# Four closing units of matmuls in four iterations in a row, with the last overflow's sum ahead of the first

## The chip, the cores and the metric

The kernel runs on one core of one Trainium2 chip. The time is the device time of one execution in microseconds; lower is better. Before the change it is 2095.76 us, the median of three runs (2090.75 to 2101.2).

The engines named here are TensorE (PE in the profile; PEld is its loading of weights), VectorE (DVE), ScalarE (ACT), GpSimd (POOL) and SyncE (SP). Each takes its instructions in the order in which the program gives them, and waits on semaphores of the others. Transfers are issued on SP's queue, and the scatters on POOL's.

## The reference

One message-passing layer of a graph network, with 6250 nodes of 128 features and 200,000 edges, sorted by `dst`:

```python
h = jnp.maximum(_layernorm(x, axis=-1), 0.0)
xw = h @ W_in
W_ij = (shifted_softplus(f_ij @ W_f1 + b_f1) @ W_f2 + b_f2) * f_ij_cutoff
x_ij = xw[dst] * W_ij                                   # one row for each edge
agg = jax.ops.segment_sum(x_ij, src, num_segments=6250)
out = x + shifted_softplus(agg @ W_o1 + b_o1) @ W_o2 + b_o2
```

`f_ij` has 20 values for each edge, `f_ij_cutoff` one. The gather goes by the sorted index `dst`, the sum by the unsorted index `src`.

## The kernel before

**The loop.** Edges are taken in 391 quads of 512. An order written out by hand (a loop over an iteration number `i`, up to 404) puts the stages of several quads side by side: in iteration `i`, quad `i` enters its first layer, quad `i-1` its second, and so on. Other work hangs on hooks: `at(i, point, fn, ...)` files a function under an iteration and a point in it, and `run(i, point)` issues what is filed there, in the order of filing. The points of one iteration stand in the order L, D0, D1, A0, A1, DM, PE2, A2, D2, S. The instructions of an engine stand in the order in which the functions were issued.

**Two ways to sum.** 237 plain quads are summed by indirect DMAs that add rows to accumulators in DRAM (`scatter`, L421, 948 transfers on POOL's queue). The other 154 quads (`mpq`, gaps of 2 and 3) go another way. The edges of such a quad are sorted by a permutation matmul into 16 groups of nodes with 32 places each, 392 nodes to a group, and are kept as tiles `mst`. What finds no place in its group is overflow, up to 64 edges a quad.

**Units.** Eight quads form a round; the last round has ten (368 to 390). When its quads are sorted, a round is summed in four units `s`, each for four groups of nodes:

- `unit_oh` (L609), VectorE: for each quad a one-hot `so`, 128 x 392. There are ten buffers for `so`, so those of the next unit in the last round go into the same ten.
- `unit_pe` (L624), TensorE: for each quad, three parts of the values and four groups, a matmul of 32 rows by 392 columns; 120 in a unit of the last round. Four PSUM banks `un`, one for each group, collect them over the whole unit.
- `unit_evac` (L635), VectorE: four additions of the banks onto `accT`, the sum in SBUF.

They are filed at `k-1` D2, `k` PE2 and `k+1` D1, where `k` comes from `unit_slots`. For the last round, whose last quad is 390, the four `k` are 396, 398, 400 and 402.

**Overflow.** Two quads share one overflow (the last: 388 and 390). After the index (`over_idx`, L562) and a diagonal matrix `dg` (L567, ScalarE), `over_row` (L575, TensorE) makes `orow`; `over_eq` (L580, VectorE) compares it to `oeq`; `over_sum` (L585, TensorE) adds edges of the same node into `osum`; `over_copy` (L590, ScalarE), `over_ji` (L595, VectorE) and `over_int` (L599, ScalarE) make rows and index; `over_scatter` files one scatter. For quad 390 `over_row` is at 397 and `over_sum` at 399: `clear(i, units)` moves a number past iterations that have a unit. So on TensorE the order is unit 0, `orow`, unit 1, `osum`, unit 2, unit 3; on VectorE ten one-hots, four additions, ten one-hots, `oeq`, four additions, ten one-hots, `ojd`, four additions, ten one-hots, then two of the last four additions.

**PSUM.** `un`, `orow` and `osum` are tiles of one tag, "B", with four buffers that are given out in turn: a tile gets the bank of the tile four places before it, and its first matmul waits until that one has been read.

**Behind it.** The number of trips of a loop for edges outside of the gather windows is read on every engine (L1009), and the loop's branch (L1010) has a barrier of all engines, which also waits until the scatters have landed. Here there are no trips. VectorE's L1009 stands behind the second of the last four additions; the other two come after the branch. Then the tail loads the DRAM accumulators (L1080), adds them to `accT`, and does the two output layers for 13 groups of 512 nodes.

The places of the change, with the hooks of the units:

```python
                k = clear(q + 8, units)
                at(k, "PE2", over_sum, q)
...
            for s, k in enumerate(unit_slots(mpq, r)):
                at(k - 1, "D2", unit_oh, r, s)
                at(k, "PE2", unit_pe, r, s)
                at(k + 1, "D1", unit_evac, r, s)
```

Of the kernel before, what the change touches and what calls it, by code (L numbers as in the profile page):

```python
# [48 lines left out]
def tile_gnn(ctx: ExitStack, tc: tile.TileContext, x, fB, cT, srcT, srcr, dstr, win_, wf1, wf2, bias, bo1c, wo1,  # L49
# [25 lines left out]
    mpq = sorted_quads(NQ)  # L75
    mpi = {q: n for n, q in enumerate(mpq)}
    units = unit_its(mpq)
# [596 lines left out]
    with tc.manual_schedule():  # L674
# [106 lines left out]
        def at(i, point, fn, *a):  # L781
            hooks.setdefault((i, point), []).append((fn, a))
# [121 lines left out]
        for r in range(-(-len(mpq) // RKQ)):  # L904
            i = mpq[RKQ * r]
            at(i - 5, "D2", rank_group, r)
            k = clear(i - 4, units)
            at(k, "PE2", rank_count, r)
            at(k + 1, "D0", rank_own, r)
            k = clear(k + 1, units)  # L910
            at(k, "PE2", rank_over, r)
            at(k + 1, "D0", rank_slot, r)
        for q in mpq:
            at(q + 1, "D2", perm_oh, q)
            at(q + 2, "D2", part_rem, q, 1)
            at(q + 2, "D2", part_rem, q, 2)
            for s in range(4):
                at(q + 3 + s // 2, "PE2", permute, q, s)
                at(q + 4 + s // 2, "A0", perm_out, q, s)
            at(q + 4, "PE2", over_pe, q)  # L920
            at(q + 5, "A0", over_out, q)
            if q == mpq[-1] and mpi[q] % 2 == 0:
                at(q + 4, "D2", over_none, q)
            if mpi[q] % 2 or q == mpq[-1]:
                at(q + 5, "DM", over_idx, q)
                at(q + 6, "A0", over_dg, q)
                k = clear(q + 6, units)
                at(k, "PE2", over_row, q)
                at(k + 1, "D0", over_eq, q)
                k = clear(q + 8, units)  # L930
                at(k, "PE2", over_sum, q)
                at(k + 1, "A0", over_copy, q)
                at(k + 1, "DM", over_ji, q)
                at(k + 1, "A2", over_int, q)
                at(k + 1, "S", over_scatter, q)
        last = mpq[-1]
        for r in range(len(mpq) // RND):
# [4 lines that stand above are left out]
# [68 lines left out]
    with tc.For_i(0, trips, 1) as ci:  # L1010
# [49 lines left out]
        s = wk.tile([P, P], F32, bufs=1, tag="dg", name="fs")  # L1060
# [112 lines left out]
def sorted_quads(nq):  # L1173
    qs, q = [], MP0
    while q < nq - MPEND:
        qs.append(q)
        q += MPGAPS[(len(qs) - 1) % len(MPGAPS)]
    return qs if len(qs) % RND <= EXTRA else qs[:len(qs) // RND * RND]
# [7 lines left out]
def unit_slots(qs, r):  # L1186
    last = len(qs) // RND - 1
    nxt = [qs[n] + 2 for n in range(RND * (r + 1), min(RND * (r + 2), len(qs) if r < last else 0)) if qs[n] - qs[n - 1] == 3]
    return nxt[:4] if nxt else [qs[-1] + 6 + 2 * s for s in range(4)]


def unit_its(qs):
    return {i for r in range(len(qs) // RND) for i in unit_slots(qs, r)}


def clear(i, busy, n=1):
    while any(i + k in busy for k in range(n)):
        i += 1
    return i
# [114 lines left out]
```

## Time and profile before

| | |
|---|---|
| median of three runs | 2095.76 us |
| profiled execution, its own time | 2098.49 us |
| span of its instructions | 2096.7 us |
| mean granted clock of TensorE | 0.977 |
| busy share of the span: PE / DVE / ACT / POOL | 92 / 84 / 85 / 81 % |
| from the first matmul of the last round's unit 0 to the barrier's end | 2007.42 to 2041.90 us |
| from there to the end of the span | 54.8 us |
| last scatter issued on POOL until | 2035.32 us |

A line of the timeline gives start and length in us, engine, line of the kernel, operation, the tile written and the tiles read, shapes, and how often it came in a row; in brackets how long the engine was idle before it, and what ended that. Times of matmuls are modelled at their ends. A row of waits gives the total in us, how often, and the longest. A row of windows gives for a stretch the busy time of each engine with its count of instructions, the clock that TensorE was granted (1.00 is full), the share of the DMA engines and GB/s.

### The profile page before, as it was taken

The numbers are of one execution on the slowest core, as the hardware profiler recorded it, in microseconds if no ns is written. First come the engines' busy times: TensorE is split into PE (matmuls) and PEld (weight loads), VectorE is DVE, ScalarE is ACT, GpSimd is POOL, SyncE is SP. The second block draws the span as 40 slices with busy tenths as digits, with TensorE's granted clock in tenths as the row PEclk, the third lists the DMA queues.
The fourth block names the chain that finished last, engine by engine and source line by source line (L and its number), as shares of the span: only waits on it lengthen the run. The fifth ranks groups of instructions, "written<-read, shape, count | busy, mean of one in ns | idle before, by whom it ended". The sixth has DMA issues, their size and how long they took to land. (4 is left out here: it accounts for less than half of the span.)

```text
span 2096.7 us, 57222 instructions
## 1 busy us (share of the span) xinstructions
PE 1925.7 (92%) x19917; PEld 1404.4 (67%) x19917; DVE 1770.8 (84%) x4749; ACT 1792.0 (85%) x4789; POOL 1690.0 (81%) x1077
## 2 busy tenths in 40 slices
PE   3788999999999999998999999999999999999976
PEld 2566667676666667666667677776777776676744
DVE  4768888898989998888888989888988988888955
ACT  4688889898989888998889999989999998898824
POOL 3677888888888888888888888888888888888864
PEclk9789999999999999999999999999999999999997
DMA  7886667676667667766766776767776667667639
GB/s 260 211 167 112 126 112 128 121 126 123 117 124 128 113 119 131 124 117 124 132 115 113 123 121 120 118 119 119 119 127 118 126 111 123 117 114 138 127 37 241
DMA packets 377588, 270.57 MB, mean 129 GB/s; under 512 B 97199, under 2 KB 337242, under 8 KB 377298
## 3 DMA queue, kind: packets, MB, share of 16 engines
q0 software_dynamic: 149200, 73.79, 36.7%
q1 hardware_dynamic: 227810, 193.04, 33.2%
q8 instruction: 157, 2.57, 0.5%
q14 instruction: 133, 1.09, 0.2%
q10 hardware_dynamic: 288, 0.07, 0.0%
HBM read 153.14 MB, written 113.59 MB: 127 GB/s over the span
## 5 line engine op out<-in xcount | busy, mean ns | idle before, releaser
L421 POOL DMA_INDIRECT acc<-s,ji x948 | 1523.7, 1607 | 327.6 <-issue 217.8
L356 ACT ACTIVATE xc<-xg,cb 128x128 f32<-128x128 f32 x1564 | 446.5, 374 | 76.7 <-PE xg L343 59.9
L531 PE MATMUL pq<-pt,pm 128*128 128x387 bf16 x2464 | 485.7, 337 | 23.0 <-ACT s L381 13.0
L351 PE MATMUL W<-w,a 128*128 128x128 f32 x3128 | 463.6, 292 | 0.0
L351 PEld LDWEIGHTS W<-w,a 128*128 128x128 f32 x3128 | 388.0, 195 | 41.7 <-issue 2.0
L624 PE MATMUL un<-so,mst 32*128 32x392 bf16 x7392 | 358.7, 331 | 38.2 <-DVE pr L471 14.9
L531 PEld LDWEIGHTS <-pm 128*128 128x128 bf16 x2464 | 240.8, 98 | 184.1 <-issue 29.4
L624 PEld LDWEIGHTS <-mst 32*128 32x128 bf16 x7392 | 229.4, 94 | 162.8 <-issue 61.3
L328 DVE SCALAR_TENSOR_TENSOR a<-z,e 128x512 f32<-128x512 f32 x391 | 267.3, 684 | 64.2 <-ACT e L304 34.5
L304 ACT ACTIVATE e<-e,con 128x512 f32<-128x512 f32 x391 | 282.3, 722 | 12.7
L373 PEld LDWEIGHTS pp<-m,eq 128*128 128x128 f32 x1896 | 253.7, 196 | 35.0 <-DVE accT L635 15.8
L373 PE MATMUL pp<-m,eq 128*128 128x129 f32 x1896 | 260.6, 281 | 14.0 <-DVE accT L635 9.2
L537 ACT CAST mst<-pq 128x387 bf16<-128x387 f32 x616 | 264.2, 480 | 6.8 <-PE pq L531 5.6
L299 ACT ACTIVATE e<-e 128x512 f32<-128x512 f32 x391 | 246.5, 630 | 12.4
L298 ACT ACTIVATE e<-z 128x512 f32<-128x512 f32 x391 | 242.2, 620 | 15.1 <-PE z L293 14.6
L381 ACT COPY s<-pp 128x258 f32<-128x258 f32 x474 | 165.4, 392 | 67.0 <-PE pp L373 30.2
L361 DVE TENSOR_TENSOR m<-W,xc 128x512 f32<-128x512 f32 x237 | 162.5, 686 | 60.1 <-ACT xc L356 46.6
L521 DVE TENSOR_TENSOR pt<-pt 128x512 f32<-128x512 f32 x308 | 212.7, 691 | 0.0
L507 DVE TENSOR_SCALAR pm<-iot,pos 128x576 bf16<-128x576 f16 x616 | 201.4, 389 | 0.0
L635 DVE TENSOR_TENSOR accT<-un,accT 128x392 f32<-128x392 f32 x288 | 142.7, 558 | 45.7 <-PE un L624 28.2
L361 DVE TENSOR_TENSOR pt<-W,xc 128x512 f32<-128x512 f32 x154 | 106.1, 689 | 81.9 <-ACT xc L356 56.4
L293 PE MATMUL z<-ft,ws 123*128 123x512 bf16 x391 | 152.1, 389 | 14.9 <-POOL b2rep L763 9.2
(156 smaller groups left out, 2716.9 us busy)
## 6 DMA issues: line engine op xcount, KB each, us to landing
rb<-reld SPq DMA_DIRECT2D x391, 64.0 KB
fsd<-f SPq DMA_DIRECT2D x49, 480.0 KB
ft<-fsd SPq DMA_DIRECT2D x195, 120.0 KB
sb<-src SPq DMA_DIRECT2D x153, 128.0 KB
fb<-in_fB_dram SPq DMA_DIRECT2D x49, 320.0 KB
ft<-fsd SPq DMA_DIRECT2D x195, 80.0 KB
acc<-s,ji POOLq DMA_INDIRECT x948
wn<-tab SPq DMA_DIRECT2D x782, 15.8 KB
```

The lines of the kernel that those rows point to most:

```text
L298: nc.scalar.activation(e, st[q]["z"], AF.Abs)
L299: nc.scalar.activation(e, e, AF.Exp, scale=-1.0)
L304: nc.scalar.activation(e, e, AF.Ln, bias=half, scale=0.5)
L328: nc.vector.scalar_tensor_tensor(a, st[q]["z"], 0.0, st[q]["l"], op0=ALU.max, op1=ALU.add)
L351: nc.tensor.matmul(W[:, c, :], st[q]["a"][:, c * P:(c + 1) * P], w2, start=False, stop=(c == 3))
L356: nc.scalar.mul(xc[:, c, :], st[q]["xg"][:, c, :], late["c", q // CQ][:, 4 * (q % CQ) + c:4 * (q % CQ) + c + 1])
L361: nc.vector.tensor_tensor(m[:, :, :P], st[q]["W"], st[q]["xc"], op=ALU.mult)
L373: nc.tensor.matmul(pp[:, c, :129], st[q]["eq"][:, k, :], m[:, k, :129], start=True, stop=True)
L421: nc.gpsimd.indirect_dma_start(out=accs[k][:, :], out_offset=bass.IndirectOffsetOnAxis(ap=ji, axis=0), in_=s, in_offset=None, compute_op=A ...
L531: nc.tensor.matmul(t[:, :PW], mp[q]["pm"][:, c, s * P:(s + 1) * P], high(mp[q]["pt"][:, c:c + 1, :PW])[:, 0], start=(c == 0), stop=(c == 3))
L537: nc.scalar.copy(mp[q]["ms", s][:, :PW], mp[q].pop(("q", s))[:, :PW])
L624: nc.tensor.matmul(ts[g][:, :GN], mp[q]["ms", s][v, k * P:(k + 1) * P], mp[q]["oh"][v], start=(q == qs[0] and k == 0), stop=(q == qs[-1] a ...
```

## The change

Two lines. The last round's four units are filed at 397, 398, 399 and 400 in place of 396, 398, 400 and 402. And for the last quad, 390, `over_sum` is filed at `q + 7` = 397 without looking for an iteration that has no unit; hooks of one point run in the order of filing, and those of the overflow are filed first, so it stands before unit 0's matmuls. Since 396 no longer has a unit, `over_row` of quad 390 moves from 397 to 396.

```diff
-                k = clear(q + 8, units)
+                k = clear(q + 8, units) if q < mpq[-1] else q + 7
                 at(k, "PE2", over_sum, q)
                 at(k + 1, "A0", over_copy, q)
                 at(k + 1, "DM", over_ji, q)
...
-    return nxt[:4] if nxt else [qs[-1] + 6 + 2 * s for s in range(4)]
+    return nxt[:4] if nxt else [qs[-1] + 7 + s for s in range(4)]
```

The instructions are the same ones. On TensorE the order becomes `orow`, `osum`, unit 0, unit 1, unit 2, unit 3. On VectorE it becomes ten one-hots, `oeq`, ten one-hots, four additions, `ojd`, ten one-hots, four additions, ten one-hots, then six additions: the one-hots of a unit stand ahead of the additions of the unit before it. Up to quad 390's last sorting matmuls nothing moves, and the order on ScalarE, POOL and SP is what it was; VectorE's L1009 still stands behind the second of the last unit's additions.

## The prediction

> **What bounds the kernel now.** The change touches only the work after the last edges, so I asked first what that work holds up. The chain that ended last begins, in order of time, with the sync queue leaving the branch of L1010 and issuing the tail's loads of the accumulators (start us, us, what):
>
> ```profile
> 2041.90 0.02 SPq L1010
> ...
> 2042.18 0.37 SPq L1080
> ```
>
> So all that follows, 55 us up to 2096.7, is counted from 2041.90. The waits of the sync queue between 1990 and 2060 us say what it stood for there (total, times, longest):
>
> ```profile
> SPq L1010 <- DMA acc<-os,oji: 33.8, 1, 33.8
> SPq L1010 <- DVEq L1009: 3.9, 1, 3.9
> ```
>
> The last scatter had landed 3.9 us before the release, near 2037.9; what ended last was VectorE reaching its own L1009. VectorE alone, from 2006 to 2042 us (start, us, engine, line, operation, tiles, count, idle before and who ended it):
>
> ```profile
> 2006.99 2.52 DVE L609 TENSOR_SCALAR so<-iot,mst 128x392 bf16<-128x392 f16 x10
> 2012.77 1.98 DVE L635 TENSOR_TENSOR accT<-un,accT 128x392 f32<-128x392 f32 x4 [3.26 <-PE un L624]
> 2014.67 2.49 DVE L609 TENSOR_SCALAR so<-iot,mst 128x392 bf16<-128x392 f16 x10
> 2017.08 0.34 DVE L580 TENSOR_SCALAR oeq<-orow,ovs 128x128 f32<-128x128 f32 x1
> 2024.00 1.99 DVE L635 TENSOR_TENSOR accT<-un,accT 128x392 f32<-128x392 f32 x4 [6.57 <-PE un L624]
> 2033.36 1.99 DVE L635 TENSOR_TENSOR accT<-un,accT 128x392 f32<-128x392 f32 x4 [4.86 <-PE un L624]
> 2035.26 2.40 DVE L609 TENSOR_SCALAR so<-iot,mst 128x392 bf16<-128x392 f16 x10
> 2040.80 1.04 DVE L635 TENSOR_TENSOR accT<-un,accT 128x392 f32<-128x392 f32 x2 [3.13 <-PE un L624]
> ```
>
> One-hots, matmuls, additions, one unit after another; L1009 stands behind the second addition of the last unit, so the release comes 1.10 after 2040.80. TensorE in the same stretch:
>
> ```profile
> 2007.42 5.15 PE L624 MATMUL un<-so,mst 32*128 32x392 bf16 x120 [0.83 <-DVE so L609]
> 2013.49 0.46 PE L575 MATMUL orow<-dg,onesf 128*128 128x128 f32 x2 [0.92 <-DVE accT L635]
> 2015.04 0.34 PE L624 MATMUL un<-so,mst 32*128 32x392 bf16 x3 [1.09 <-DVE so L609]
> 2017.47 6.63 PE L624 MATMUL un<-so,mst 32*128 32x392 bf16 x117 [2.09 <-DVE oeq L580]
> 2024.62 0.49 PE L585 MATMUL osum<-mo,oeq 128*128 128x132 f32 x2 [0.51 <-DVE accT L635]
> 2026.27 6.84 PE L624 MATMUL un<-so,mst 32*128 32x392 bf16 x120 [1.15 <-DVE so L609]
> 2035.63 5.16 PE L624 MATMUL un<-so,mst 32*128 32x392 bf16 x120 [2.53 <-DVE so L609]
> ```
>
> Two things are to be seen. Unit 1 stops after three matmuls: its fourth tile gets the bank of `orow`, which `oeq` reads, and `oeq` stands on VectorE behind ten one-hots. And units 0 and 3 take 5.15 us (43 ns a matmul), units 1 and 2 about 1.6 more. The windows tell why (window, length, PE busy, PEld, DVE, ACT, POOL, granted clock, DMA); their edges are where the clock changed:
>
> ```profile
> 2013.80:2017.20 3.40, 0.49 (x5) 0.19 (x4) 3.40 (x14) 0.00 (x0) 2.79 (x3) 0.99 0.36 34
> ...
> 2024.00:2027.43 3.43, 1.76 (x31) 1.21 (x34) 3.43 (x11) 0.27 (x1) 2.82 (x3) 0.99 0.44 38
> 2027.43:2030.85 3.42, 3.42 (x51) 2.13 (x44) 1.07 (x5) 0.29 (x1) 2.81 (x3) 0.51 0.38 32
> ...
> 2034.26:2037.67 3.41, 2.04 (x52) 1.48 (x55) 3.40 (x13) 0.00 (x0) 1.07 (x1) 1.00 0.37 35
> 2037.67:2041.10 3.43, 3.12 (x76) 1.98 (x68) 0.30 (x1) 0.00 (x0) 0.00 (x0) 1.00 0.00 0
> ```
>
> The clock changes on a grid of about 3.41 us. After a window with 0.49 or 1.76 us of matmuls the next runs at half clock; after one with 2.04 it does not.
>
> **The change, step by step.** *The overflow's sum in front.* `orow` (L575) now comes before unit 0, `osum` (L585) directly behind it, and unit 0 behind both. `dg` ends on ScalarE at 2007.51 (row of L567: 2007.11, 0.40); `orow` takes 0.46, to about 2008.0. But `oeq` stands on VectorE behind unit 0's ten one-hots. Before, it began 2.41 after the first of the ten (2014.67 to 2017.08); so now 2006.99 + 2.41 = 2009.40, done with its 0.34 at 2009.74. `osum` starts 0.05 later, as the matmul of 2017.47 did after `oeq`: 2009.79. Unit 0's fourth tile takes the bank of `osum`, free when the copy `os` is done: it began 0.53 after `osum` (2024.62, 2025.15) and takes 0.27, so 2010.59. With 0.06 to react the fourth matmul stands at 2010.65, and the other work at full clock, 117 x 0.043 = 5.03, ends at 2015.68. Before it ended at 2012.57: **3.11 lost**. Cover for the ten one-hots is gone: TensorE used to work under them.
>
> *Units in a row.* The ten one-hots of the next unit now stand before the additions of this one. They write the ten buffers this unit reads, so the tenth waits for its last matmul, and the additions queue behind it. A cycle, from the last matmul of a unit to that of the next: 0.20 until VectorE reacts (2012.57 to 2012.77), 0.24 for the tenth one-hot, 1.98 for four additions, since the fourth matmul needs the fourth bank, 0.06, and 5.03: **7.51**. Before, from the additions of unit 2 to those of unit 3: 2040.80 - 2033.36 = 7.44. Nothing is won: the one-hots were hidden already, as the first was enough to start the matmuls, and the bound is the four banks.
>
> *The stall of unit 1* goes: it stopped between 2015.04 and 2017.47, worth 2.43 less 3 x 0.043 = **2.3 won**.
>
> *Scatter, copies, index.* `ojd`, `oji` and the scatter move forward, but POOL issues its queue back to back (1.85 each) in the same order until 2035.32, and no DMA changes place in it or on SP: nothing. If the index were late it would cost POOL only after 2033.78; it is ready some 10 us earlier.
>
> *Sum at full clock.* After: 2015.68 + 3 x 7.51 + 0.20 = 2038.41 for the last additions. Before, taking out the two slow units (6.63 - 5.03 = 1.60 and 6.84 - 5.15 = 1.69): 2040.80 - 3.29 = 2037.51. At equal clock the change loses 0.9.
>
> *The clock* is the unknown. I lay the new times on this profile's grid. Window 2006.97 to 2010.38 holds `orow`, `osum` and three matmuls, about 1.0 us: half clock until 2013.80, which takes 1.57 off unit 0's progress; it ends at 2017.26. The next window, to 2020.60, holds three trickling matmuls and 0.86 of unit 1, whose fourth is at 2019.74: about 1.0, so half clock until 2024.04, 1.72 lost, end 2026.46. Unit 2's fourth is at 2028.94; its window holds 2.0, nearest to the row with 2.04: held. End 2033.97. Unit 3's fourth is at 2036.45, its window has 1.35: half clock, 1.71 lost, end 2043.20. Additions at 2043.40: **2.6 later than 2040.80**. Bounds: no drop, 2038.41, 2.4 earlier; a drop in all four units, 6.7, so 2045.1, 4.3 later. Below, the landed scatter (2037.9) caps any gain at 3.9. I take 2.6: every gap between units is now some 2.4 us, and the gaps of 4.9 and 2.2 (with `osum` in it) dropped while that of 2.5 did not.
>
> The Trainium skill (TensorE: Matmul & The Clock Gate, HAM oscillation) gives as its rule that the clock falls after idle gaps of more than about 3.4 us. This trace differs: in the window that ended at 2027.43 no gap passed 1.15 us and the clock fell. By the rule, with `orow` and `osum` splitting the gap before unit 0, no unit would be slow and the last additions would stand at 2038.41; by the rows, at 2043.40. Its Part 1 says the grid runs free of the kernel, so another execution would lay it elsewhere; one profile here cannot show that.
>
> **The rivals.** *The clock holds.* For it: the gap of 2.53 before unit 3 cost nothing. Against: three new gaps and a worse one before unit 0. Price -2.4. *The clock drops in every unit* (slower): the place is each unit's first window, the price 1.6 to 1.7 each, 4.3 in all, decided where a window holds under some 1.8 to 2.0 us of matmuls; my unit 2 stands just on that edge. *Half clock throughout:* should no window reach the limit, 480 x 0.043 = 20.6 comes on top of 2038.41, 18.2 later. Against it: at half clock matmuls fill more of a window, and here every slow window was followed by a full one. *The stage is not the gate:* if the last scatter landed after VectorE, nothing would move; it had 3.9 us to spare.
>
> **How the numbers follow.** The profiled execution took 2098.49 with a span of 2096.7; the median of the three runs is 2095.76 (2090.75 to 2101.2), 2.7 below it. On that execution: 2096.7 + 2.6 = 2099.3 of span, 2101.1 in all; on the median 2098.4. About 0.5%, 10.5 us, is what a measurement of this kernel can tell from no change, and no likely case gets there. Chances: forecast (1 to 3.5 later) 0.60, 2098.4; clock holds 0.17, 2093.4; drops everywhere 0.18, 2100.1; half clock throughout 0.02, 2114; gate elsewhere 0.03, 2095.8. Range: 2093.4 less and 2100.1 plus 3, some half of the three runs' spread: 2090.5 to 2103. The forecast's own is 2094 to 2102. Chance of slower by over 0.5%: 0.05 (half clock, and a spread of runs on top of the late cases); faster 0.02 (spread alone, as 3.9 is the cap); same 0.93.
>
> **What would show it.** In the new profile `osum` at about 2.8 us after unit 0's first one-hot, unit 0's first matmul 3 us later than now, no stall on `oeq` inside a unit, four additions ending in each cycle of about 7.5 us where the clock is full, and at least two units with a half-clock window. Wrong it would be if TensorE started unit 0 before `osum`, if the next unit's matmuls began ahead of the additions, or if the release at L1010 were ended by the scatter.

## The result and the profile after

The changed kernel takes 2099.22 us, the median of 20 runs (2092.34 to 2103.41), against 2093.59 for the kernel before in 20 runs (2087.5 to 2101.2). The ratio is 1.0021 with a 95% interval of [1.0012, 1.003]: 4.4 us slower, 2.5 to 6.3 by the interval, which is less than the 0.5% that was taken as the bound of a change. The profiled execution took 2099.24, with a span of 2097.3.

The single spans say little, since one kernel's executions differ by more than ten microseconds. So I measure from a point inside: from the first of unit 0's one-hots (2006.99 before, 2006.03 after) to the start of the last unit's additions, called the stage here. It was 33.81 us and is 35.17.

The waits of the sync queue after, from 1990 to 2060 us (total, times, longest):

```profile
SPq L1010 <- DMA acc<-os,oji: 34.2, 1, 34.2
...
SPq L1010 <- DVEq L1009: 5.4, 1, 5.4
```

VectorE still ends last, and by 5.4 us where it was 3.9: the place of the bound is as forecast. VectorE after:

```profile
2006.03 2.52 DVE L609 TENSOR_SCALAR so<-iot,mst 128x392 bf16<-128x392 f16 x10
2008.47 0.34 DVE L580 TENSOR_SCALAR oeq<-orow,ovs 128x128 f32<-128x128 f32 x1
...
2017.52 1.96 DVE L635 TENSOR_TENSOR accT<-un,accT 128x392 f32<-128x392 f32 x4
...
2024.94 1.97 DVE L635 TENSOR_TENSOR accT<-un,accT 128x392 f32<-128x392 f32 x4
...
2034.16 1.96 DVE L635 TENSOR_TENSOR accT<-un,accT 128x392 f32<-128x392 f32 x4
2041.20 1.04 DVE L635 TENSOR_TENSOR accT<-un,accT 128x392 f32<-128x392 f32 x2 [5.07 <-PE un L624]
```

The first additions stand 11.49 us after the first one-hot, where before they stood 5.78 after it. From there on a cycle is 7.42 where the clock is full (2017.52 to 2024.94), as the last one was before (7.44). TensorE after:

```profile
2008.87 0.49 PE L585 MATMUL osum<-mo,oeq 128*128 128x132 f32 x2 [1.77 <-DVE oeq L580]
2009.29 0.34 PE L624 MATMUL un<-so,mst 32*128 32x392 bf16 x3
2010.36 6.81 PE L624 MATMUL un<-so,mst 32*128 32x392 bf16 x117 [0.73 <-ACT os L590]
...
2019.53 5.13 PE L624 MATMUL un<-so,mst 32*128 32x392 bf16 x117 [0.15 <-DVE accT L635]
...
2026.96 6.81 PE L624 MATMUL un<-so,mst 32*128 32x392 bf16 x117
...
2036.18 5.13 PE L624 MATMUL un<-so,mst 32*128 32x392 bf16 x117
```

`osum` comes 2.84 after the first one-hot, as forecast (2.8). But unit 0's fourth matmul comes 4.33 after it, not 3.66 as the prediction has it (2010.65 less 2006.99): the copy of the sum was late. ScalarE, and then GpSimd, in the same stretch:

```profile
2010.04 0.27 ACT L590 COPY os<-osum 128x132 f32<-128x132 f32 x1 [3.31 <-DMA acc<-os,oji]
```

```profile
2006.64 1.62 POOL L421 DMA_INDIRECT acc<-os,oji  x1 [0.30 <-ACT dg L567]
```

The copy waited for a DMA, not for the sum. `os` has two buffers, so the last overflow's rows go where those of the overflow of quads 378 and 380 lie, and that one's scatter, in the back of a full queue, was issued only at 2006.64 and had to land. Its issue ended at 2008.26, and the copy began 1.78 later. Units 0 and 2 are slow after the change, as units 1 and 2 were before. Windows on the clock's grid (columns as before):

```profile
2007.60:2011.00 3.40, 1.40 (x21) 0.87 (x25) 1.21 (x5) 0.27 (x1) 2.79 (x3) 1.00 0.33 25
...
2024.60:2028.00 3.40, 2.06 (x32) 1.02 (x34) 2.56 (x6) 0.00 (x0) 2.79 (x3) 1.00 0.44 38
...
2034.87:2038.30 3.43, 2.98 (x55) 1.73 (x57) 1.25 (x3) 0.00 (x0) 0.00 (x0) 1.00 0.16 17
```

After the first two the clock is half (0.50 and 0.51 in the window that follows), after the third it stays. 2.06 us of modelled busy time dropped here where 2.04 had held before; the count of matmuls separates these two better (32 against 52).

### The profile page after: what moved, and what is told of

It reads as the page before. It is cut to its first block, busy times and chain, and to the rows that moved or that the text cites. A ratio compares the mean times of both kernels' runs of the same rounds, so it can differ in the third digit from the quotient of the medians.

```text
span 2097.3 us, 57252 instructions
## 1 busy us (share of the span) xinstructions
PE 1926.7 (92%) x19917; PEld 1402.2 (67%) x19917; DVE 1777.3 (85%) x4749; ACT 1794.7 (86%) x4789; POOL 1688.1 (80%) x1077
## 5 line engine op out<-in xcount | busy, mean ns | idle before, releaser
L609 DVE TENSOR_SCALAR so<-iot,mst 128x392 bf16<-128x392 f16 x616 | 166.1, 335 | 10.5 <-PE un L624 10.2
```

## The experiments

"Fourth" is the start of unit 0's fourth matmul after the first one-hot. "At full clock" is the stage less what each slow unit took over 5.13 us for 117 matmuls or 5.15 for 120. "Scatter" is the end of the last scatter's issue on POOL, "loads" the first load of the tail, both after the first one-hot. All in us, from one profile each; the ratio is over the runs, 12 of each kernel and 20 of the changed one.

| kernel | fourth | slow units | stage | at full clock | scatter | loads | ratio to before |
|---|---|---|---|---|---|---|---|
| before | | 1, 2 | 33.81 | 30.62 | 28.33 | 35.19 | |
| before_again | | 1, 2 | 34.08 | 30.95 | 30.51 | 35.47 | 1.0010 [0.9998, 1.0022] |
| after | 4.33 | 0, 2 | 35.17 | 31.81 | 28.15 | 36.55 | 1.0021 [1.0012, 1.003] |
| after_again | 6.37 | 0, 1 | 36.71 | 33.69 | 30.17 | 38.10 | 1.0026 [1.0012, 1.004] |
| spaced | 6.27 | 0, 1 | 36.76 | 33.72 | 30.15 | 38.14 | 1.0025 [1.0009, 1.0041] |
| flag_only | 5.01 | 0, 2 | 36.27 | 32.63 | 28.91 | 37.66 | 1.0023 [1.0006, 1.004] |
| os_three | about 4.0 | 0, 1, 3 | 35.79 | 30.92 | 28.13 | 37.17 | 1.0005 [0.999, 1.0019] |
| sum_second | 3.06 | 1 | 32.07 | 30.39 | 32.06 | 34.64 | 1.0000 [0.9986, 1.0015] |
| warm | 4.56 | none | 32.30 | 32.30 | 28.59 | 37.63 | 1.0023 [1.0006, 1.004] |
| warm_flag | 5.04 | none | 32.71 | 32.71 | 29.01 | 34.10 | 1.0003 [0.9989, 1.0017] |
| banks | 3.9 | | 25.50 | | 25.28 | 27.83 | 0.9992 [0.998, 1.0004] |
| banks_sum_second | 3.21 | 0 | 26.99 | | 27.11 | 29.80 | 0.9992 [0.9978, 1.0005] |
| best_again | 3.03 | none | 25.23 | | 25.36 | 28.01 | 0.9992 [0.9979, 1.0005] |

In os_three and banks no break shows before the fourth matmul; there the figure is the end of the copy plus 0.06.

**Both kernels once more.** No edit.

> The changed kernel once more, for a second trace. Stage length here means: from the first of unit 0's one-hots to the start of the last unit's additions; it was 33.81 us before and 35.17 after. Late start theory (unit 0 waits for the overflow's sum; the cycles are unchanged; the clock falls at random): unit 0's fourth matmul again 3.7 to 4.4 us after the first one-hot, three cycles of 7.4 us where the clock is full, stage 34 to 37 by how many units meet the half clock, ratio to before 1.001 to 1.003. Rival (the loss lies outside of the stage, in the loop or the tail): the stage is no longer than before's 33.8 and the ratio is above 1.001 all the same.

> The kernel before once more, for a second trace of it: stage 33.8 plus or minus 1.7 by the half-clock units (unit 1 always one of them), unit 1 stopped after three matmuls until the comparison is done, ratio 1.000. If the stage of one and the same kernel scatters by more than 2 us, a difference of 1.4 between two single traces says little.

The stage of before repeats within 0.3 us, with the same two slow units. That of the changed kernel does not: 36.71 against 35.17. ScalarE and then TensorE of after_again:

```profile
2007.49 0.27 ACT L590 COPY os<-osum 128x132 f32<-128x132 f32 x1 [5.33 <-DMA acc<-os,oji]
```

```profile
2007.82 6.47 PE L624 MATMUL un<-so,mst 32*128 32x392 bf16 x117 [2.04 <-ACT os L590]
```

The same wait, longer: the old scatter was issued 2.55 us after the first one-hot here, and 0.61 after it in the first trace. GpSimd of after_again:

```profile
2004.00 1.62 POOL L421 DMA_INDIRECT acc<-os,oji  x1 [0.30 <-issue]
```

The wait cost the fourth matmul 2.7 us beyond the forecast 3.66, not 0.67, and 6.37 is outside of the 3.7 to 4.4 that were expected. The ratio of 1.0010 for two equal kernels shows what a ratio of 12 runs leaves open.

**A third buffer for `os`.**

```diff
-        s = sp_.tile([P, 132], F32, tag="os", name="os", bufs=2)
+        s = sp_.tile([P, 132], F32, tag="os", name="os", bufs=3)
```

> A third buffer for the rows of an overflow, so that the copy of the sum does not wait for an older scatter that still reads its buffer. Theory: the copy starts 0.5 us after the sum's start instead of 1.17, unit 0's fourth matmul stands at 3.6 to 3.7 us after the first one-hot instead of 4.33, and the stage is 0.6 to 0.7 shorter at equal clock. Rival (the copy waited for the sum itself, or the fourth matmul for something else): it stays at 4.3.

ScalarE and then TensorE of os_three:

```profile
2004.32 0.27 ACT L590 COPY os<-osum 128x132 f32<-128x132 f32 x1 [2.98 <-PE osum L585]
```

```profile
2004.21 6.66 PE L624 MATMUL un<-so,mst 32*128 32x392 bf16 x120
```

The copy now waits for the sum, and unit 0 runs through without a stop. The fourth matmul came at about 4.0, not at the 3.6 to 3.7 expected: the sum itself met the half clock, and the copy began 0.85 us after its start where 0.5 was expected. At full clock the stage is 30.92, 0.9 to 2.8 below the changed kernel's two traces and within the span of before's. As measured it is 35.79 because three units met the half clock, which the edit does not choose. So this trace shows the wait gone and not a shorter stage; that time was won rests on the runs. In the time it has 1.0005 beside 1.0026 on the same chip (medians 2094.38 and 2099.35); the two intervals overlap a little.

**The sum behind unit 0.**

```diff
-                k = clear(q + 8, units) if q < mpq[-1] else q + 7
+                k = clear(q + 8, units) if q < mpq[-1] else q + 8
```

> The units stay in a row, but the last overflow's sum stands behind unit 0, ahead of unit 1. Late start theory: unit 0's fourth matmul waits only until the comparison behind the ten one-hots is done, 2.8 us after the first one-hot in place of 4.33, and the sum costs nothing between the units since additions end later than the copy; the stage is 1.5 us shorter than after's at equal clock, some 33.6, or 30.3 to 35.3 with no to three more half-clock units. Rival (it is units in a row, one-hots ahead of additions, that cost): cycles of more than 7.8 us at full clock and a stage of 35 or more, as in the changed kernel.

TensorE and then the sync queue's waits of sum_second:

```profile
2002.17 0.34 PE L624 MATMUL un<-so,mst 32*128 32x392 bf16 x3
2004.24 5.13 PE L624 MATMUL un<-so,mst 32*128 32x392 bf16 x117 [1.73 <-DVE oeq L580]
2010.26 0.49 PE L585 MATMUL osum<-mo,oeq 128*128 128x132 f32 x2 [0.89 <-DVE accT L635]
```

```profile
SPq L1010 <- DMA acc<-os,oji: 37.9, 1, 37.9
```

Unit 0's first three matmuls run early, the fourth waits for `oeq` alone (3.06; 2.8 was expected), and the sum between the units costs nothing. The units are in a row as in the changed kernel, with cycles of 7.43 and 7.06 at full clock, and the loss is gone: 30.39 at full clock, and a ratio of 1.0000 beside 1.0026 on the same chip (medians 2095.58 and 2099.35; these intervals overlap a little too). Here VectorE is no longer the last: the scatter holds the barrier, and the row for VectorE is missing from the waits.

**Units two iterations apart, the sum still in front.**

```diff
-    return nxt[:4] if nxt else [qs[-1] + 7 + s for s in range(4)]
+    return nxt[:4] if nxt else [qs[-1] + 7 + 2 * s for s in range(4)]
...
-        for i in range(max(NQ + 7, last + 14, r0_end + 2)):
+        for i in range(max(NQ + 7, last + 15, r0_end + 2)):
```

> The sum stays in front of unit 0, but the units stand two iterations apart (397, 399, 401, 403), so that a unit's additions come ahead of the next unit's one-hots as before the change. Late start theory: unit 0's start as in the changed kernel (4.3), cycles of 7.4 to 7.5 at full clock, so the stage is within 0.5 us of the changed kernel's at equal clock: 34 to 37. Rival (units in a row cost): the stage is 1 us or more below the changed kernel's at equal clock. Rival (units in a row gain and hide the late start): cycles of 7.8 or more here.

The stage at full clock is 33.72, the changed kernel's second trace has 33.69; a cycle at full clock is 7.44 (additions at 2029.90 and 2037.34). The copy waited for the old scatter here too (5.24 us, up to 2006.53), so the fourth matmul came at 6.27 where 4.3 was expected. In these traces it makes no difference whether a unit's one-hots stand before or behind the additions of the unit ahead of it. The loss goes with the sum in front, and by os_three most of it with the buffer that the copy waits for.

**TensorE kept busy in the gaps.** Matmuls into a bank that nobody reads.

```diff
+    def filler(n):
+        t = ps.tile([P, 512], F32, tag="A", name="fill", bufs=4)
+        for _ in range(n):
+            nc.tensor.matmul(t, onesb, b2rep.rearrange("k c f -> k (c f)"), start=True, stop=True)
...
         mp[q]["row"] = t
+        if q == mpq[-1]:
+            filler(8)
...
         un[r, s] = ts
+        if r == len(mpq) // RND - 1 and s < 3:
+            filler(9)
```

> The changed kernel with matmuls that nobody reads in TensorE's gaps: eight of 128 x 512 between the last overflow's row and its sum, nine after each of units 0, 1 and 2. They add work and leave nothing out. Clock theory (the granted clock falls after a window of 3.4 us with under some 1.8 to 2.0 us of matmuls): all four units run at full clock, 117 matmuls in 5.0 to 5.2 us, three cycles of 7.4, stage 31.7 to 32.2 against 35.17; release held by VectorE until about 2 us before the scatters would hold it. Rival (the slow units come from something else than idle windows): units of 6.8 us are still there. Rival (the fillers themselves are in the way): cycles above 7.8.

No unit was slow and the stage was 32.30, just above the 31.7 to 32.2 expected. The time gained nothing: 1.0023. The loads came 5.3 us behind the start of the last additions in place of 1.4, because VectorE computed the flag (the number of trips that L1009 reads) only after the last additions, at 2045.29. By the code the fillers' tile takes a place in the ring of banks that the flag's tile is also given from; that this is what put the flag back was not shown apart. So the run was made again with the flag's instructions at fixed places in iterations 391 and 392, and beside it the changed kernel with nothing but that.

> A control: the changed kernel with nothing but the flag's instructions moved into the loop's last iterations, as in the runs with the other banks; the units stay in four banks. Theory (the flag's place is worth nothing): ratio 1.001 to 1.003 as for the changed kernel, fourth matmul of unit 0 4.3 to 6.4 us after the first one-hot, stage 34 to 38, release held by VectorE. Rival (moving the flag is what made the runs with the other banks faster): ratio at or below 1.000.

> The run with matmuls that nobody reads, again with the flag's instructions moved forward, since in the first such run the flag was computed only behind the last additions and the release came 5.1 us after them in place of 1.1. Clock theory: all units at full clock, stage 32 to 34.5 by the wait of the copy, release 1.1 us after the last additions or at the scatter's landing, ratio 1.000 to 1.0015: better than the control by the 3 us of its half-clock units. Rival (the clock is not worth anything in the run's time): ratio as the control's, 1.002 or more.

The flag's place alone is worth nothing (1.0023, as the changed kernel). With the fillers the ratio is 1.0003; the two intervals overlap, the medians on the same chip are 2101.70 and 2096.69. TensorE of warm_flag, units 1 to 3:

```profile
2023.75 5.60 PE L631 MATMUL un<-so,mst 32*128 32x392 bf16 x120
...
2031.34 5.61 PE L631 MATMUL un<-so,mst 32*128 32x392 bf16 x120
...
2038.93 5.49 PE L631 MATMUL un<-so,mst 32*128 32x392 bf16 x120
```

These include the trickle of the first three matmuls, and none is near 6.8. The slow units are the idle windows' doing, and the half clock is worth 3.6 us of this stage (36.27 against 32.71). That is a gain beside the change and not the cause of its loss: the kernel before has two slow units as well.

**Units 1 and 3 in the other four banks**, which nothing uses by then; the flag's instructions again at fixed places.

```diff
-            t = ps.tile([P, 512], F32, tag="B", name="un", bufs=4)
+            tag = "A" if s % 2 and r == len(mpq) // RND - 1 else "B"
+            t = ps.tile([P, 512], F32, tag=tag, name="un", bufs=4)
```

> The changed kernel with units 1 and 3 of the last round in the other four PSUM banks, which are free by then; the flag's few instructions move into the loop's last iterations to make that possible. Theory (the cycle is bound by four banks that must be added before the next unit may write them): TensorE goes from unit to unit without a gap, cycles of 5.2 us, no half clock after unit 0, stage about 25 to 27 us. Then the last scatter holds the release: it falls 2 to 4 us earlier than before's relative to the first one-hot (34.9), not 8, and the time is 2 to 4 us below before's, ratio 0.998 to 0.999. Rival (the cycle is bound by one-hots and additions on VectorE): cycles of 7 or more. Rival (VectorE stays the gate): release 8 us or more earlier, ratio 0.996.

> Both: units 1 and 3 in the other banks and the last overflow's sum behind unit 0. Theory: unit 0 starts 1.5 us earlier than in the run with the banks alone, the stage is 23.5 to 25.5 us, but the release is held by the last scatter, so the time is the same within 0.5 us of that run's. Rival (VectorE is still the gate): 1.5 us faster than that run.

> Units 1 and 3 in the other banks and the sum behind unit 0, once more for a closer interval. Theory (the last scatter holds the release, so the gain over before is what VectorE came later than it, 2 to 4 us): ratio 0.998 to 0.9995, release 2.2 to 2.6 us after the last scatter's issue ends. Rival (no gain over before): 1.000 or more.

TensorE and then the sync queue's waits of banks:

```profile
2013.88 22.16 PE L625 MATMUL un<-so,mst 32*128 32x392 bf16 x480
```

```profile
SPq L1022 <- DMA acc<-os,oji: 29.6, 1, 29.6
```

All 480 matmuls run as one, so the cycle was bound by the four banks. The stage falls by some ten microseconds, the time by less: the scatter holds the barrier, and the loads start 2.55 after the last scatter's issue in this run. On one chip the medians are 2101.70 for flag_only and 2095.55 for best_again. Three runs, one with the sum in front and two with it behind unit 0, gave 0.9992 each, and each interval reaches past 1. They are clear of the changed kernel's interval, and not shown to be faster than before. Two expectations missed: in banks the loads came 7.4 us earlier after the first one-hot than before's 35.19, where 2 to 4 were expected, because the last scatter's issue ended at 25.28 and not near 28.33; and in banks_sum_second the stage was 26.99, above 23.5 to 25.5, with unit 0 at half clock from its fourth matmul on.

## Why the prediction was right

The bound and the direction came out: VectorE's arrival at the barrier, later rather than earlier. The time lies near too, 2098.4 forecast and 2099.22 measured, but part of that is luck. 2098.4 is 2.6 us on top of 2095.76, the median of three runs; over 20 runs the kernel before has 2093.59. The change itself is 4.4 us [2.5, 6.3], above the forecast's own case of 1 to 3.5. By its steps:

- *`orow` and `osum` in front:* the mechanism held, the term was too small. 3.11 was forecast for the later end of unit 0. Its additions, less what the half clock took (1.68 and 1.34), stood 9.81 and 11.77 us after the first one-hot against 5.78 before: 4.0 and 6.0, where 3.11 and the tenth one-hot's 0.24 make 3.35. The rest, 0.7 and 2.6, is the copy's wait for an old scatter, shown by the third buffer. The prediction took the copy's 0.53 us behind the sum from a row 18 us into the stage, when that scatter had long landed; the change moved the copy to little more than 3 us, and there the scatter had been issued only at 0.61 or at 2.55. POOL's queue was looked at for its order, not for what its backlog still holds.
- *Units in a row:* 7.51 forecast, 7.42 and 7.43 measured, and no difference when spaced. Right.
- *The stall of unit 1 gone*, worth 2.3: no unit after the first stops on `oeq` any more. From the first additions to the second it is 7.42, where it was 11.23 less 1.50 for the slow unit, 9.73: 2.3 won. Right.
- *At full clock* 0.9 later was forecast. Two traces each: 31.81 and 33.69 against 30.62 and 30.95, on average 2.0 later. Without the copy's wait it would be less than forecast: os_three has 30.92. The last two cycles, 7.54 and 7.04 at full clock, took 0.5 less than before's 7.67 and 7.44, which the prediction did not foresee.
- *The clock:* three slow units, 0, 1 and 3, were laid out against two; the traces of the changed kernel have two each, 0 and 2, then 0 and 1. So the 1.7 us forecast for one more was wrong, and on average the copy's wait, which the prediction put at nothing, took its place: two errors that nearly cancelled, by luck. The grid does not follow the kernel: reckoned back from the half-clock windows, its first edge behind the first one-hot came 3.3 us after it before, 1.5 after the change and 2.3 in after_again, so the old profile's grid could not tell which unit is hit. The stage was forecast 2.6 longer; the traces have it 2.0 longer on average (35.94 against 33.95).
- *The rule of clock and gaps:* against the rule of long gaps the rows decided rightly: in the window from 2024.60 of the trace after, the longest stop of TensorE was 0.89 us and the clock fell. The limit of 1.8 to 2.0 us of busy time that the prediction read from the rows did not hold: 2.06 dropped here, and 1.38 held in spaced (the last section has the row).
- *The rivals:* the clock that holds, with a gain, did not come. The drop in every unit, at 4.3, has the measured size, but no trace with the sum in front has four slow units (os_three has three; after, after_again, spaced and flag_only have two). That every slow window is followed by a full one is so in before's stage, not everywhere: in after_again the clock is half for two windows in a row (6.83 us from 2003.75). The scatter as the gate came in no trace of the changed kernel, but it had only 3.9 and 2.2 us to spare in the two traces of before, and it does hold the barrier in sum_second and the runs with the other banks.

What stays open: the runs say 4.4 us [2.5, 6.3], the stages of two traces each 2.0. From the first load to the end of the span it is 54.7 us in both traces after, 54.5 and 54.2 before, so the traces give some 2.3 in all. The interval's lower end and the traces do not quite meet; how the copy's wait and the slow units are spread over executions was not measured beyond these traces.

## What to carry to other kernels

Before moving a step forward in front of a long run of matmuls, follow it to the buffer it writes last, and ask which transfer still reads that buffer: a full DMA queue holds it long after its data were ready, and the wait lands on whatever now stands behind the step. And measure a short stage from a point inside the trace, at one clock, since executions of the same kernel scatter by far more than the stage can change.

## What the runs showed of the hardware

The granted clock fell without any long gap. In the windows of 3.41 us on the clock's grid that lie in the stages of the eleven traces without fillers, up to 32 of the units' matmuls dropped it and 36 or more held it. Three rows (columns as before), the first of spaced, the second of best_again and the third of sum_second:

```profile
2030.13:2033.55 3.42, 1.38 (x36) 1.00 (x39) 3.42 (x12) 0.00 (x0) 0.60 (x1) 1.00 0.25 25
...
2012.39:2015.80 3.41, 1.72 (x34) 1.02 (x36) 2.67 (x11) 0.00 (x0) 2.80 (x3) 1.00 0.42 38
...
2009.13:2012.54 3.41, 2.31 (x34) 1.25 (x33) 2.49 (x7) 0.27 (x1) 2.89 (x2) 1.00 0.44 38
```

After the first two the clock stayed at 1.00, after the third it was 0.50. Of the 34 in each of the last two rows, two are those of `orow` or `osum`, so at 32 of the units' both happened. Neither the modelled busy time nor the longest stop decides: 2.31 us dropped and 1.38 held, and the first row holds a stop of 2.04 us, where 0.89 was the longest in the window that dropped in the trace after. Idle pieces that add up are enough. What exactly is counted is not shown; the limit is read off these windows alone.

Filling the idle pieces with matmuls that nobody reads gave back 3.6 us of a stage of 36.3 (flag_only and warm_flag, one trace each).
